# A fused transformer kernel on one core: where the first attention's joins, ternary signs, a weight sum and one tile of values stand

## The chip, the cores and the metric

The kernel runs on one core of a Trainium2 chip. A core has five engines that run side by side, each with its own instruction queue: TensorE (PE, matmuls and transposes; PEld is its loading of weights), VectorE (DVE), ScalarE (ACT), GpSimd (POOL) and SyncE (SP, which issues most of the transfers). An engine works through its queue in order; a wait at the head of a queue holds everything behind it. Matmuls write to PSUM; the other working memory is SBUF.

The metric is the device time of one execution in microseconds (us). Before the change three runs took 573.16, 573.84 and 576.12 us; the median is 573.84.

## What is computed

Four layers, each an attention and a feed-forward, are added onto one residual `x` (2 x 256 rows of 256). Each addition is scaled by the tanh of a gate, and each block's input is layer-normalised. The change touches the first layer and the start of the second:

```python
x = x + jnp.tanh(g_xattn[0]) * _L0_xattn_ref(_layernorm(x, axis=-1), ctx_2048)
x = x + jnp.tanh(g_ffn[0]) * _L0_ffn_ref(_layernorm(x, axis=-1), L0_ffn_W_up, L0_ffn_W_gate, L0_ffn_W_down)
x = x + jnp.tanh(g_xattn[1]) * _L1_xattn_ref(_layernorm(x, axis=-1), ctx_2048, L1_xattn_Wq, L1_xattn_Wk, L1_xattn_Wv, L1_xattn_Wo)
```

The first attention has 16 heads per batch entry and no weights: the queries are slices of the normalised `x`, the keys and values slices of the context. The first feed-forward has ternary weights:

```python
scale = jnp.mean(jnp.abs(w)) + EPS
q = jnp.clip(jnp.round(w / scale), -1.0, 1.0) * scale
...
hidden = jax.nn.silu(up) * gate
return jnp.einsum('bse,de->bsd', hidden, wd)
```

Three weight matrices (up, gate, down) are so reduced to signs of -1, 0 or 1 and one scale each. The second attention has 16 heads of width 128 with query, key, value and output weights.

## The kernel before, in words

`x` is held as four tiles of 128 rows (n = 0 to 3). The first attention runs as a pipeline of 18 steps s, four for each tile (n = s // 4): in each step TensorE computes scores (`l0_scores`, L450), ScalarE takes their exponentials (L456), and TensorE multiplies the exponentials of the step before with the values (`l0_values`, L464). TensorE's instructions are kept in the order of the text by `in_turn`. VectorE's and GpSimd's in this stage are kept in the order of the text too, each in its own list, by `inline` with `line` and `pool_line`, which tie each instruction behind the one before it.

A tile's values come in two halves, each in a PSUM tile of its own; there are two such buffers, so a new half waits until an older one has been read. `l0_join` (L473 for the first half, L475 for the second) brings the halves together in SBUF on VectorE, two instructions each. Then `l0_exchange` (L479) swaps parts of it between partitions with one matmul, and `l0_finish` takes a reciprocal of the result (L485), multiplies and adds to `x` (L489, L280). `norm_stats` follows for the feed-forward's layernorm (L217, L218 on VectorE, L219, L220 on GpSimd), and `norm_apply` (L236) writes the normalised row tile `xn0`.

The ternary weights are prepared between these steps. `ternary_sum` (L339, VectorE) sums the absolute values of one weight matrix over a 128 x 2048 tile; a matmul with ones (L344) adds over the partitions, and `ternary_scale` (L348 to L350) makes the scale and the bounds. `ternary_below` (L360, GpSimd) compares half a matrix with the lower bound; `ternary_signs` (L367, VectorE) compares it with the upper bound and subtracts. So there are six signs, two for each matrix, each 128 x 1024. Before the change they are made in pairs: after the first joins of tiles 1, 2 and 3, ahead of these tiles' second joins. The sum of the down weights (the third) stands ahead of tile 1's first join.

After the last step comes `l1_values_of(0, ...)`: the values of the second attention's first group of four heads, in eight tiles (two matmuls each, L277, and a copy by ScalarE, L564). They depend on the context and the weights alone. Seven are in the text ahead of the feed-forward; the eighth stands behind the feed-forward's norm. In `ternary_ffn` the normalised tiles are transposed on TensorE (L248) and each is split into a high and a low part (`split`: L778, L780 on VectorE, L779 on ScalarE). Then come the matmuls with the signs, silu (L804), product (L805), the split of the product (L372 VectorE, L373 ScalarE, L374 GpSimd) and the matmuls with the down signs (L793). The result is transposed (L816) and added to `x` (L818).

The second attention starts with two heads' keys (L277, copied at L573), the norm of `x` (`norm_pair`, then L236), its transposes (L248, copied at L834 by ScalarE into `xT`), the queries of the first heads and the first scores. The transposes of both norms, and some of the key products (L696), share two PSUM buffers, `ps_tr`. Where the text does not tie instructions, a scheduler orders those of an engine.

All weights live in twelve slots of one SBUF tile, `slab`. The down weights lie in slot 4, up and gate in slots 10 and 11. `load_group(2)` and `load_group(3)` (L101, on SP's queue) bring the second attention's third and fourth weight groups into slots 4 to 7 once these are read for the last time.

Of the kernel before, what the change touches and what calls it, by code (L numbers as in the profile page):

```python
# [22 lines left out]
ALU = mybir.AluOpType  # L23
# [26 lines left out]
def flamingo(ctx: ExitStack, tc: tile.TileContext, a: dict, out: bass.AP):  # L50
    nc = tc.nc
# [53 lines left out]
    l0_w = [load(10, "l0_up"), load(11, "l0_gate")]  # L105
# [71 lines left out]
    def behind(i, j, reason):  # L177

        tc.add_manual_dep(i.ins, j.ins.name, mybir.DependencyInfo(
            mybir.DependencyClass.NoSync, mybir.DependencyReason.DATA), reason=reason)  # L180
# [24 lines left out]
    def inline(i, line=line):  # L205
        if line:
            if line[-1] is not None:
                behind(i, line[-1], "in the order of the text")
            line[:] = [i]
        return i  # L210
# [24 lines left out]
    def norm_apply(n, xn, stats):  # L235
        inline(nc.vector.tensor_scalar(xn[:, n, :], x[:, n, :], *stats, ALU.subtract, ALU.mult))  # L236
# [16 lines left out]
    def tokens(t, n):  # L253
        return t[:, n // 2, :, n % 2 * P : (n % 2 + 1) * P]
# [80 lines left out]
    signs, scales, bounds, parts = [], [], [], []  # L335

    def ternary_sum(w):
        part = small.tile([P, 1], F32, tag="tq", name="tq_part")
        inline(nc.vector.tensor_reduce(part, w, AX.X, ALU.add, apply_absolute_value=True))  # L339
        parts.append(part)  # L340
# [19 lines left out]
            inline(nc.gpsimd.tensor_scalar(t, wi, sc[:, 2:3], None, ALU.is_lt), pool_line)  # L360
            below.append((wi, sc, t))

    def ternary_signs():
        for _ in range(2):
            wi, sc, t = below.popleft()
            signs.append(q4.tile([P, 1024], F32R, tag="q4", name="signs"))
            inline(nc.vector.scalar_tensor_tensor(signs[-1], wi, sc[:, 1:2], t, ALU.is_gt, ALU.subtract))  # L367

    def halves(hi, lo, v):

# [126 lines left out]
    for s in range(18):  # L497
        n = s // 4
        if s < 16:
            es[s] = l0_scores(n, s // 2 % 2, s % 2)  # L500
        if s < 2:

            in_turn(nc.tensor.matmul(busy, lhsT=ones, rhs=ones, start=True, stop=True))

        if s % 4 == 2 and n or s == 17:
            done = n - 1
            l0_exchange(mixed[done], acc[done, 1], done == 1)
        if 1 <= s <= 16:
            m, i, half = (s - 1) // 4, (s - 1) // 2 % 2, (s - 1) % 2
            if half == 0:  # L510
                acc[m, i] = ps_acc.tile([P, 2, D], F32, tag="acc", name="acc")
            l0_values(m, i, half, es.pop(s - 1), acc[m, i][:, 0, :])
        if s == 0:
            ternary_sum(l0_w[0])
            ternary_sum(l0_w[1])
        if s == 3:
            behind(nc.scalar.activation(tg, graw, AF.Tanh), exps[-3], "with the table of exponentials")
            p = acc[0, 0][:, 1, :]
            for w in range(2):
                in_turn(ternary_total(p[:, w : w + 1], w))  # L520
            for w in range(2):
                ternary_scale(p[:, w : w + 1])
            ternary_below(0)
            value_columns(1)
            queries([2], rest[:1])
        if s % 4 == 2 and n or s == 17:
            r = l0_finish(done, acc[done, 1], mixed[done], done == 1)
            stats[done] = norm_stats(done)
            if done == 0:
                ternary_sum(l0_w[2])  # L530
            inline(nc.gpsimd.tensor_add(all_t, all_t, sums.pop(0)), pool_line)
            l0_pool = inline(nc.gpsimd.tensor_add(all_r, all_r, r), pool_line)
            if done < 2:
                ternary_below(done + 1)
        if s % 4 == 2 and s < 16:
            mixed[n] = q2.tile([P, 2, D], F32, tag="q2", name="mixed")
            l0_join(0, acc[n, 0][:, 0, :], mixed[n])
            if n == 0:
                rest = [norm_stats(m) for m in (2, 3)]
            else:  # L540
                ternary_signs()
        if s % 4 == 0 and s:
            l0_join(1, acc[n - 1, 1][:, 0, :], mixed[n - 1])
            if n == 1:
                queries([3], rest[1:])
            if n > 1:
                norm_apply(n - 2, xn0, stats[n - 2])
    norm_apply(3, xn0, stats[3])
    line.clear()
    pool_line.clear()  # L550
    l0_psum.close()
# [6 lines left out]
    def l1_values_of(g, tiles):  # L558
        v = slab[:, 8 + 2 * (g % 2) : 10 + 2 * (g % 2), :].rearrange("p s (m c) -> p (s m) c", m=4)
        for mt in tiles:  # L560
            p = mm()
            chain(p, [(ctxT[:, mt // 4, k, mt % 4 * P : (mt % 4 + 1) * P], l1_w[g][2][:, k, :])
                      for k in range(2)])
            nc.scalar.copy(v[:, mt, :], p)  # L564
        return v

    def l1_keys_of(h):
        kT = q4.tile([P, B * M], F32, tag="q4", name="kT")
        for b in range(B):
            p = mm()  # L570
            chain(p, [(l1_w[h // 4][1][:, k, (h % 4) * HD : (h % 4 + 1) * HD], ctxT[:, b, k, :])
                      for k in range(2)])
            nc.scalar.copy(kT[:, b * M : (b + 1) * M], p)  # L573
        return kT


    v_next = l1_values_of(0, range(7))

# [190 lines left out]
    def ternary_ffn():  # L771


        xs = [q4.tile([P, B, 2, 256], F32R, tag="q4", name="xs") for _ in range(2)]

        def split(n, tr):
            top = q1.tile([P, 2, P], F32, tag="q1", name="topx")
            nc.vector.tensor_scalar(top.bitcast(I32), tr.bitcast(I32), -4096, None, ALU.bitwise_and)  # L778
            nc.scalar.copy(tokens(xs[0], n), top)  # L779
            nc.vector.tensor_sub(tokens(xs[1], n), tr, top)  # L780

        norm_tiles(split, xn0)
        l1_values_of(0, [7])
        s2 = small.tile([P, 1], F32, tag="s2", name="s2", bufs=1)
        nc.vector.tensor_mul(s2, scales[1], scales[2])
        nc.vector.tensor_mul(s2, s2, gf(0))
        outs = [ps_acc.tile([P, T], F32, tag="acc", name="outT") for _ in range(2)]

        def l0_down(c, h):
            w = signs[4 + c // 4].rearrange("p (c d) -> p c d", d=D)[:, c % 4, :]  # L790
            for dh in range(2):
                for i in range(2):
                    nc.tensor.matmul(outs[dh], lhsT=w[:, dh * P : (dh + 1) * P], rhs=h[:, i, :],  # L793
                                     start=(c == 0 and i == 0), stop=(c == 7 and i == 1))

        ps = {}
        for c, _, ts in by_batch(FCH):
            if c not in ps:
                ps[c] = mm(), mm()
            for w, p in zip((0, 2), ps[c]):  # L800
                chain(p[:, ts], [(signs[w + k][:, c * P : (c + 1) * P], batch(h, k, ts)) for k in range(2) for h in xs])
            if ts.stop == T:
                s = q2.tile([P, T], F32, tag="q2", name="silu")
                nc.scalar.activation(s, ps[c][0], AF.Silu, scale=scales[0])  # L804
                nc.vector.tensor_mul(s, s, ps[c][1])  # L805
                h = q4.tile([P, 2, T], F32R, tag="q4", name="hT")
                halves(h[:, 0, :], h[:, 1, :], s)
                later(lambda c=c, h=h: l0_down(c, h), 1)
        flush()
        for dh in range(2):  # L810
            p = outs[dh]
            o = q2.tile([P, T], F32, tag="q2", name="o0")
            nc.scalar.copy(o, p)
            tr = ps_tr.tile([P, NT, P], F32, tag="tr", name="tr")
            for n in range(NT):
                nc.tensor.transpose(tr[:, n, :], o[:, n * P : (n + 1) * P], ident)  # L816
            cols = x[:, :, dh * P : (dh + 1) * P]
            nc.vector.scalar_tensor_tensor(cols, tr, s2, cols, ALU.mult, ALU.add)  # L818
# [3 lines left out]
    ternary_ffn()  # L822
    l1_w += [load_group(2), load_group(3)]
    keys = deque(l1_keys_of(h) for h in range(2))


    line.append(None)
# [76 lines left out]
    for g in range(4):  # L904
        v, oTs = v_next, []
        if g < 3:
            v_next = values_of[g + 1]
        for hl in range(4):
# [15 lines left out]
            for b in range(B):  # L924
                es, by_ones, t = l1_scores(b, qT, kT, h > 13)
# [179 lines left out]
    last = norm_stats(NT - 1)  # L1105
# [67 lines left out]
    halves = slice(0, 2), slice(2, 4)  # L1173
# [94 lines left out]
    last = nc.scalar.activation(prob, lgt, AF.Exp, scale=-1.0)  # L1268
# [19 lines left out]
    t, u = rtile(), place  # L1288
# [20 lines left out]
    for n in range(NT):  # L1309
# [9 lines left out]
    _, owners = nc.values_load_multi_w_load_instructions(  # L1319
        owner_i[0:1, :], engines=[mybir.EngineType.SP], min_val=0, max_val=E - 1,  # L1320
        skip_runtime_bounds_check_because="a count, cut at 7")
# [10 lines left out]
    top = rtile((P, NT))  # L1332
    inline(nc.vector.reduce_max(top, prob, axis=AX.X))
    t = rtile()
# [221 lines left out]
    es, t = l3_exps(0, ps3[0])  # L1556
# [909 lines left out]
```

## Time and profile before

The profile is of one execution, which took 572.92 us; the span from its first to its last instruction is 571.2 us. TensorE's granted clock was 0.999 of full.

| engine | busy us | share of the span |
|---|---|---|
| PE | 553.1 | 97% |
| PEld | 401.0 | 70% |
| DVE | 371.9 | 65% |
| ACT | 178.7 | 31% |
| POOL | 216.4 | 38% |

Busy time of each engine in the stretches that the change touches, in us:

| stretch (us from the start) | what runs there | PE | DVE | ACT | POOL |
|---|---|---|---|---|---|
| 27 to 35 | first attention, tile 1 ends | 6.30 | 7.43 | 6.30 | 7.67 |
| 35 to 44 | tile 2 | 9.00 | 8.53 | 6.70 | 6.30 |
| 44 to 53 | tile 3 | 7.27 | 8.58 | 3.58 | 8.92 |
| 53 to 66 | values tiles, norm of the feed-forward | 13.00 | 5.80 | 4.75 | 6.76 |
| 66 to 92 | first feed-forward | 26.00 | 11.72 | 13.65 | 12.04 |
| 92 to 99 | norm of the second attention | 6.06 | 5.10 | 3.06 | 4.70 |

A line of the timeline gives the start, the duration (from the first start to the last end where instructions are merged, x4 for four of them), the engine, the line of the kernel, the operation, output<-input by the program's names and, in brackets, how long the engine had been idle before it and what ended that. One matmul instruction on fp32 data shows as two records. In the chain of work that ended last each piece is a start, a length, an engine, a tile's name and a line. "L12" is line 12 of the kernel.

### The profile page before, as it was taken

Reading aid. Unit: us, or ns where it says so; the run is one execution under the profiler, and the core shown is the slowest. Engines: PE = TensorE matmul, PEld = TensorE weight load, DVE = VectorE, ACT = ScalarE, POOL = GpSimd, SP = SyncE. Lnnn points to the kernel's source line nnn. Section 1 sums busy time; section 2 is a strip of 40 time slices with the busy share of each in tenths; the row PEclk is TensorE's granted clock in tenths of the full one; section 3 lists DMA queues with packets and bytes.
Section 4 is the critical chain, followed back from the end, with each engine's and each line's share of the span. In section 5 each row is a group of like instructions: output and inputs, shape, how many; then the busy total and the mean of one; then the engine's idle time right before and its main releaser. Section 6 shows DMA issues by size and latency. Waiting matters only on the chain.

```text
span 571.2 us, 8750 instructions
## 1 busy us (share of the span) xinstructions
PE 553.1 (97%) x3300; PEld 401.0 (70%) x3300; DVE 371.9 (65%) x744; ACT 178.7 (31%) x329; POOL 216.4 (38%) x368
## 2 busy tenths in 40 slices
PE   8988999999999999999999999999999999999996
PEld 6553675778788787887878786887775555884445
DVE  6998444677867888588885895675567434563323
ACT  5874543422222222123222221331323221432221
POOL 3787456626332464134342344702022001252151
PEclk9999999999999999999999999999999999999999
DMA  7904200002002100102032324272020899704013
GB/s 294 412 18 188 107 0 1 0 1 74 1 0 75 43 32 1 37 37 75 0 118 104 117 94 158 75 239 75 0 75 2 338 419 415 170 33 129 18 53 116
DMA packets 15528, 59.15 MB, mean 104 GB/s; under 512 B 2653, under 2 KB 5924, under 8 KB 11846
## 3 DMA queue, kind: packets, MB, share of 16 engines
q1 hardware_dynamic: 13430, 53.70, 25.7%
q0 software_dynamic: 1472, 4.28, 2.3%
q8 instruction: 28, 0.46, 0.3%
q10 hardware_dynamic: 576, 0.53, 0.3%
q14 instruction: 22, 0.18, 0.1%
HBM read 53.70 MB, written 5.25 MB: 103 GB/s over the span
## 4 chain that ended last, share of the span: by engine, by line
PE 84%; DVE 8%; POOL 3%; issue 2%; ACT 1%; DMA 1%; SPq 0%; POOLq 0%; DVEq 0%; ACTq 0%
PE mm L277 22%; PE acc L277 18%; PE mm_t L646 4%; PE mm L658 4%; PE mm L1369 4%; PE mm_t L696 4%; PE mm L646 3%; PE mm_t L658 3%; PE mm L696 3%; PE acc L766 2%; PE s L450 2%; PE mm L1700 2%; PE acc L1390 2%; PE acc L1722 2%; PE acc L464 2%
## 5 line engine op out<-in xcount | busy, mean ns | idle before, releaser
L854 ACT ACTIVATE e<-mm 128x512 f32<-128x512 f32 x64 | 38.0, 597 | 115.0 <-PE mm L277 112.4
L873 DVE RECIPROCAL r<-acc 128x256 f32<-128x256 f32 x32 | 56.2, 1757 | 20.7 <-PE acc L277 20.7
L277 PE MATMUL mm<-qT,kT 128*128 128x256 f32 x256 | 61.1, 380 | 0.0
L277 PE MATMUL acc<-e,slab 128*128 128x256 f32 x256 | 60.5, 379 | 0.0
L277 PEld LDWEIGHTS acc<-e,slab 128*128 128x128 f32 x256 | 48.6, 190 | 9.2 <-issue 2.9
L875 POOL TENSOR_TENSOR all_t<-all_t,t 128x256 f32<-128x256 f32 x32 | 24.1, 753 | 80.4 <-DVE t L859 80.4
L277 PEld LDWEIGHTS mm<-qT,kT 128*128 128x128 f32 x256 | 47.7, 190 | 9.4 <-issue 2.9
L876 POOL TENSOR_TENSOR all_r<-all_r,r 128x256 f32<-128x256 f32 x32 | 23.3, 728 | 56.4 <-DVE r L873 56.4
L277 PE MATMUL mm<-xT,slab 128*128 128x256 f32 (+1 forms) x132 | 38.7, 442 | 0.3 <-DVE k L998 0.3
L456 ACT ACTIVATE slab<-s 128x1024 f32<-128x1024 f32 x32 | 30.9, 1021 | 8.5 <-PE s L450 7.9
L858 DVE TENSOR_TENSOR t<-e,e 128x512 f32<-128x512 f32 x32 | 22.9, 716 | 15.0 <-ACT e L854 14.4
L219 POOL TENSOR_TENSOR rstd<-mv,eps_ln 128x1 f32<-128x1 f32 x26 | 6.4, 245 | 68.0 <-DVE mv L218 68.0
L277 PEld LDWEIGHTS mm<-xT,slab 128*128 128x128 f32 x132 | 24.2, 190 | 10.4 <-issue 7.1
L277 PE MATMUL acc<-slab,oT 128*128 128x256 f32 x128 | 29.4, 381 | 0.5 <-DVE oT L874 0.4
L277 PE MATMUL mm<-slab,ctxT 128*128 128x512 f32 x64 | 29.0, 594 | 0.0
L280 DVE SCALAR_TENSOR_TENSOR x<-acc,tg,x 128x256 f32<-128x256 f32 x28 | 13.5, 481 | 23.6 <-PE acc L277 19.8
L277 PEld LDWEIGHTS acc<-slab,oT 128*128 128x128 f32 x128 | 23.7, 190 | 4.9 <-DVE oT L874 1.2
L864 ACT CAST th<-t 128x256 fp32r<-128x256 f32 x28 | 11.3, 405 | 45.4 <-DVE t L862 45.4
L1369 PE MATMUL mm<-slab,xsT 128*32 128x512 f32 x192 | 22.8, 596 | 0.2 <-ACT xsT L1324 0.2
L865 POOL TENSOR_TENSOR th<-t 128x256 fp32r<-128x256 f32 x28 | 20.5, 732 | 5.6 <-DVE t L862 4.6
L236 DVE TENSOR_SCALAR xn<-x,mv,rstd 128x256 f32<-128x256 f32 x28 | 14.0, 507 | 10.4 <-POOL rstd L220 10.0
L450 PE MATMUL s<-slab,ctx_nat 32*128 32x256 f32 x256 | 20.2, 401 | 0.1
(405 smaller groups left out, 1172.2 us busy)
## 6 DMA issues: line engine op xcount, KB each, us to landing
slab<-in_l_gu_all SPq DMA_DIRECT2D x16, 1024.0 KB, 5.2
slab<-in_l_all SPq DMA_DIRECT2D x4, 2048.0 KB, 10.5
slab<-in_l_dn_all SPq DMA_DIRECT2D x4, 1024.0 KB, 5.1
slab<-in_l_dn_all SPq DMA_DIRECT2D x8, 512.0 KB, 10.0
slab<-in_l_gu SPq DMA_DIRECT2D x4, 704.0 KB, 12.5
ctx_nat<-in_ctx SPq DMA_DIRECT2D x4, 512.0 KB, 8.0
slab<-in_l_up SPq DMA_DIRECT2D x2, 1024.0 KB
slab<-in_l_gate SPq DMA_DIRECT2D x2, 1024.0 KB, 10.3
```

The costliest lines, as they stand in the source:

```text
L277: inline(nc.tensor.matmul(dst, lhsT=lhsT, rhs=rhs, start=(i == 0), stop=(i == len(pairs) - 1)), pe_line)
L450: in_turn(nc.tensor.matmul(ps[j // 2][:, j % 2, k, :], lhsT=ctx_nat[rows, b, hf, c * P : (c + 1) * P], rhs=qm[rows, n, i, :], start=True, ...
L456: exps.append(nc.scalar.activation(es[d].rearrange("p j k q -> p (j k q)"), ps[d].rearrange("p j k q -> p (j k q)"), AF.Exp))
L646: nc.tensor.matmul(dst, lhsT=w, rhs=t, start=True, stop=True)
L658: nc.tensor.matmul(t[:, i, :], lhsT=w, rhs=b, start=True, stop=True)
L696: nc.tensor.matmul(dst[:, j, :], lhsT=t[:, j * P : (j + 1) * P], rhs=w, start=True, stop=True)
L854: nc.scalar.activation(e, s, AF.Exp, scale=HD ** -0.5)
L858: nc.vector.tensor_add(t, es[0], es[1])
L873: nc.vector.reciprocal(r, acc[:, 1, :])
L875: nc.gpsimd.tensor_add(all_t, all_t, t)
L876: nc.gpsimd.tensor_add(all_r, all_r, r)
L1369: inline(nc.tensor.matmul(ps[j * BLK : (j + 1) * BLK, :], lhsT=xsT[k][:, (4 * q + j) * BLK : (4 * q + j + 1) * BLK], rhs=gu2[:, home(q, j) ...
```

## The change

Five edits, all of order:

- Tile 1: the sum of the down weights moves from ahead of the first join to behind it. The two signs that followed that join are no longer made there.
- Tile 2: the pair of signs behind its first join is now the first pair (up weights).
- Tile 3: no signs between its joins. One sign (gate weights, first half) is made after its second join and the normalisation of tile 2, another (second half) after the normalisation of tile 3.
- The two signs of the down weights are made in `ternary_ffn`, behind the last instruction of the last split.
- Six of the eight values tiles stand ahead of the feed-forward's norm instead of seven, the seventh behind it, and the eighth after the keys of the second attention's first two heads.

```diff
-    def ternary_signs():
-        for _ in range(2):
+    def ternary_signs(halves, last=None):
+        for _ in range(halves):
             wi, sc, t = below.popleft()
             signs.append(q4.tile([P, 1024], F32R, tag="q4", name="signs"))
-            inline(nc.vector.scalar_tensor_tensor(signs[-1], wi, sc[:, 1:2], t, ALU.is_gt, ALU.subtract))
+            i = inline(nc.vector.scalar_tensor_tensor(signs[-1], wi, sc[:, 1:2], t, ALU.is_gt, ALU.subtract))
+            if last:
+                behind(i, last[0], "the norm is waited for")
...
             r = l0_finish(done, acc[done, 1], mixed[done], done == 1)
             stats[done] = norm_stats(done)
-            if done == 0:
-                ternary_sum(l0_w[2])
             inline(nc.gpsimd.tensor_add(all_t, all_t, sums.pop(0)), pool_line)
...
             if n == 0:
                 rest = [norm_stats(m) for m in (2, 3)]
-            else:
-                ternary_signs()
+            elif n == 1:
+                ternary_sum(l0_w[2])
+            elif n == 2:
+                ternary_signs(2)
         if s % 4 == 0 and s:
             l0_join(1, acc[n - 1, 1][:, 0, :], mixed[n - 1])
             if n == 1:
                 queries([3], rest[1:])
             if n > 1:
                 norm_apply(n - 2, xn0, stats[n - 2])
+            if n == 4:
+                ternary_signs(1)
     norm_apply(3, xn0, stats[3])
+    ternary_signs(1)
...
-    v_next = l1_values_of(0, range(7))
+    v_next = l1_values_of(0, range(6))
...
+        last_split = []
+
         def split(n, tr):
             top = q1.tile([P, 2, P], F32, tag="q1", name="topx")
             nc.vector.tensor_scalar(top.bitcast(I32), tr.bitcast(I32), -4096, None, ALU.bitwise_and)
             nc.scalar.copy(tokens(xs[0], n), top)
-            nc.vector.tensor_sub(tokens(xs[1], n), tr, top)
+            last_split[:] = [nc.vector.tensor_sub(tokens(xs[1], n), tr, top)]
 
         norm_tiles(split, xn0)
-        l1_values_of(0, [7])
+        l1_values_of(0, [6])
+        ternary_signs(2, last_split)
...
     ternary_ffn()
     l1_w += [load_group(2), load_group(3)]
     keys = deque(l1_keys_of(h) for h in range(2))
+    l1_values_of(0, [7])
```

## The prediction

> **What bounds the kernel now.** I read three views: the busy line of the page, the chain of work that ended last (what the end time hangs on), and the timelines of single engines around each place where that chain leaves TensorE. The page first:
>
> ```profile
> PE 553.1 (97%) x3300; PEld 401.0 (70%) x3300; DVE 371.9 (65%) x744; ACT 178.7 (31%) x329; POOL 216.4 (38%) x368
> ```
>
> TensorE (PE) has work for 97% of the span, and the chain lies on it for 84%, on VectorE for 8%, so a gain must come from its few gaps. The chain in time order (start, us, what) shows one in the first attention:
>
> ```profile
> 27.16 2.17 DVE tq_part L339
> 29.33 0.45 DVE mixed L473 x2
> 29.78 0.25 issue
> 30.03 2.80 DVE signs L367 x2
> 32.83 0.80 DVE mixed L475 x2
> ```
>
> The joins (L473, L475) feed TensorE; the weight sum (L339) and the signs (L367) stand ahead of them on VectorE (DVE), and nobody needs these two so early. The chain leaves TensorE in the same way for signs at 48.35 (3.09) and the join at 51.44. TensorE's own timeline (start, us, operation; idle before it and who ended that idleness):
>
> ```profile
> 28.68 1.15 PE L450 MATMUL s<-slab,ctx_nat 32*128 32x256 f32 x16
> 30.26 1.07 PE L464 MATMUL acc<-slab 128*32 128x256 f32 x16 [0.43 <-DVE mixed L473]
> 31.26 1.15 PE L450 MATMUL s<-slab,ctx_nat 32*128 32x256 f32 x16
> 33.67 0.70 PE L479 MATMUL acc<-mixed,swap 128*128 128x256 f32 x2 [1.27 <-DVE mixed L475]
> ...
> 49.03 1.98 PE L277 MATMUL mm<-slab,ctxT 128*128 128x512 f32 x4
> 52.28 0.70 PE L479 MATMUL acc<-mixed,swap 128*128 128x256 f32 x2 [1.27 <-DVE mixed L475]
> ```
>
> Three waits, all ended by a join; tile 3's joins are the last of these. Tile 2's signs (38.75, two in 2.94) cost nothing: its exchange at 43.18 did not wait.
>
> **The change, part by part.** The instruction lists of the two kernels differ in VectorE's places of one sum and six signs, and in the place of one values tile (two matmuls, shown as 4 records, and one ScalarE copy). GpSimd's list and SP's keep their order; nothing is added or removed.
>
> *Joins first.* (1) Tile 1's first join may run at 27.1, straight after the statistics, and ends by 28.0; the values matmuls then follow the scores at 28.68 + 1.07 = 29.75 (1.07 is the step where nothing waits, 21.60 to 22.67), not at 30.26: 0.51 gained. (2) The sum then runs 28.0 to 30.2, the second join to 31.0. The exchange is due after one values block (1.00) and one scores block (1.07), 29.75 + 2.07 = 31.82, so it no longer waits. Before, it came 33.67 - 31.26 - 1.07 = 1.34 after its turn: 1.34 gained. The exponentials don't step in: step 9's run 29.92 to 31.86 and are used after the exchange, 32.6. (3) Tile 3's second join needs only the last values matmuls, which end about 49.1 less the 1.85 already gained, 47.3, and ends by 48.2; the exchange is due one values tile after that block, at 49.03 + 1.72 - 1.85 = 48.90. Before: 52.28 - 50.75 = 1.53 late: 1.53 gained. Sum 3.38 (the row's own idle figures, taken from modelled ends, give 2.97; that is the lower end).
>
> *What the signs now stand before.* The third sign precedes tile 3's reciprocal, the fourth follows the last normalisation. Tile 3's chain, reciprocal to normalised row (53.02 to 58.19, 5.2 us), starts about 50.1 in the new time and ends about 55.2; its transposes come at 60.4, since TensorE has values tiles until then. That cover is 5 us; without it each sign would cost its 1.3.
>
> The fifth and sixth come after the last split, ahead of the feed-forward's first product (L805). Rows there:
>
> ```profile
> 66.37 0.74 DVE L780 TENSOR_TENSOR xs<-tr,topx 128x256 fp32r<-128x256 f32 x2
> 69.02 0.69 DVE L805 TENSOR_TENSOR silu<-silu,mm 128x512 f32<-128x512 f32 x1 [1.91 <-ACT silu L804]
> ...
> 70.25 1.30 POOL L374 TENSOR_TENSOR hT<-silu,top 128x512 fp32r<-128x512 f32 x1 [7.03 <-DVE top L372]
> ```
>
> VectorE is idle 1.91 before L805. A sign that nothing holds up takes 1.28, and the next starts 1.19 after it (38.75, 39.94); two occupy 2.38, from 67.03 to 69.41 on the old clock: the product is 0.39 late. Queued behind it are the truncation (L372), GpSimd's low half (L374) and then TensorE's L793 (first matmul at 71.61), whose second matmul, 0.23 later, at 71.84, needs that half. The half ended at 71.55, for the second chunk at 73.20 against a need at 73.42, so 0.16 to 0.23 of slack remains once about 0.06 of signalling is taken off. Stall 0.39 - 0.16, about 0.25. Ends: nothing (VectorE starts them in a gap), and 0.9 if the pair takes 3.02, as at 48.35.
>
> [...] Rows: of the six signs three take 1.60 to 1.90 with GpSimd at work beside them, three 1.27 to 1.28, and GpSimd's additions (L531, L532) take 1.65 and 1.71 beside signs, 0.73 alone. [...]
>
> *The values tile.* Six of the eight tiles, not seven, are computed ahead of the norm's transposes. Each is 4 records at 0.429 (24 records from 52.98 in 10.30): 1.72 off TensorE's path there, for rows 0 to 2 have been normalised long before the transposes at 63.12, and row 3 about 5 us before its own.
>
> It comes back in the second attention's norm, after five key matmuls. TensorE's rows there:
>
> ```profile
> 95.85 0.60 PE L248 MATMUL tr<-ident,xn 128*128 128x128 f32 x4
> 97.04 0.41 PE L248 MATMUL tr<-ident,xn 128*128 128x128 f32 x2 [0.58 <-ACT xT L834]
> 97.77 0.41 PE L248 MATMUL tr<-ident,xn 128*128 128x128 f32 x2 [0.33 <-DVE xn L236]
> 98.02 0.60 PE L696 MATMUL mm_t<-slab,ctxT 128*128 128x256 f32 x2
> 98.64 1.98 PE L277 MATMUL mm<-xT,slab 128*128 128x512 f32 x4
> ```
>
> and ScalarE's there:
>
> ```profile
> 96.05 0.59 ACT L573 COPY kT<-mm 128x512 f32<-128x512 f32 x1 [1.05 <-PE mm L277]
> 96.54 0.66 ACT L834 COPY xT<-tr 128x256 f32<-128x256 f32 x2
> ```
>
> TensorE idles 0.91 here, less than the tile's 1.72. In these rows' time: the tile runs 95.85 to 97.57, transposes 0 and 1 to 98.01. ScalarE copies the tile at 97.77 (0.2 after its last matmul, as at 63.32), with the transposes' copies queued behind it: xT 0 at 98.26 to 98.63, xT 1 to 98.92. Two PSUM buffers hold transposes, so the third waits for xT 0 (98.76, 0.13 later, as 96.91 to 97.04), the fourth for xT 1 (99.05). The key matmul behind them (98.02, 0.43) needs a buffer of the same pair, so xT 2 (0.44 after its transpose: 99.20 to 99.57): 99.70 to 100.13. The queries then start at 100.13, not 98.64: 1.49 lost. Ends: 0.81 (the tile fills the 0.91) and 2.21 (no idleness filled, and the 0.49 of the copy added); a gain is excluded, as the matmuls run there.
>
> *Transfers.* The load of the third weight group (the last L101) overwrites slot 4, which the last two signs read. It moves from 51.5 to about 64.5 on SP's queue; behind it is only a load that issues at 130.1. Its first reader is GpSimd's sum at 137.99; with the slowest landing of such a load (18.0) it lands by 83. Cost nothing, 55 us of cover.
>
> *Sum:* 3.38 + 1.72 - 0.25 - 1.49 = 3.36 gained. The profiled execution took 572.92, 0.92 below the median of 573.84: it would give 569.6; against the median, 570.5.
>
> **The rivals.** B: the tile fills the second norm's gap. For it: the trace shows 0.91 idle there; against: ScalarE's queue order. Price 0.81, gain 4.04: 569.8. C: the last signs meet GpSimd and run as at 48.35. [...] Stall 0.9, gain 2.71: 571.1. [...] D: the exchanges are no longer late through VectorE but through ScalarE's exponentials. For it: each step holds two of about 1.02 against TensorE's 2.07; against: ScalarE idled 2.22 before step 11's. It decides once under 0.02 of the 3.38 is left; then 573.9, no faster. E, the slower side: the third group's load arrives after its reader. Place SP's queue, price one for one; the reader comes at 134.6 in the new time, a landing at 138 uses up the gain and one at 141 makes 0.5% (576.7), 76 us after the issue where 18.0 is the longest seen. For it only that its issue moves by 13 us.
>
> **How the numbers follow.** About 0.5% (2.9 us) is what a measurement of this kernel can tell from no change; its three runs span 573.16 to 576.12. Forecast 0.58 (570.5, own range 569.8 to 571.2, of which three quarters lie under 570.97), B 0.14, C 0.13, D 0.10, E and the like 0.05. Faster: 0.43 + 0.14, 0.57. Slower: E 0.05 and a third of D, 0.08. Same: 0.35. The unknown prices give 2.97 + 1.72 - 0.9 - 2.21 = 1.58 at the least and 3.38 + 1.72 - 0.81 = 4.29 at the most, 572.3 to 569.5. With the runs' scatter the range is 569.3 to 573.0; it leaves out D and E, 0.15.
>
> **What would show it.** Right: no idle at TensorE ahead of the exchanges of tiles 1 and 3, L464 in the step between unidle, the first transposes of the feed-forward's norm near 58.0, its first L793 near 66.5 with the second matmul waiting 0.1 to 0.3 for GpSimd, the first queries near 95.3. Wrong: an idle gap of over 0.5 ended by an exponential, signs of 1.6 or more after the split, a wait on the third group's load, or queries whose distance from the x update differs from 7.4 (now 5.9, 92.73 to 98.64).

## The result and the profile after

Six runs of the changed kernel took 570.11 to 571.83 us, median 571.08; six of the kernel before beside them 573.13 to 576.12, median 574.14. The ratio is 0.9936, 95% interval 0.9912 to 0.9959: about 3.1 us faster, where 3.36 had been forecast. The profiled execution took 570.11 us with a span of 568.4 (before 572.92 and 571.2), at the same granted clock, 0.999.

In the changed kernel the lines of the code are a few numbers further down: the joins are now L475 and L477, scores L452, values L466, the exchange L481, the feed-forward's product L813, GpSimd's low half of its split L376, the down matmuls L801, the copies of the values tiles L569 and of the second norm's transposes L843 (the runs further down differ by a line or two). From the page, the busy line and the chain that ended last:

```profile
PE 553.2 (97%) x3300; PEld 401.6 (71%) x3300; DVE 371.9 (65%) x744; ACT 178.5 (31%) x329; POOL 214.6 (38%) x368
...
PE 91%; DVE 4%; POOL 2%; ACT 2%; issue 1%; DVEq 0%; POOLq 0%; ACTq 0%
```

The work is the same; the chain now lies on TensorE for 91% of the span instead of 84%, and on VectorE for 4% instead of 8%. TensorE's timeline in the first attention (start, us, engine, line, operation; idle before it in brackets):

```profile
28.76 1.15 PE L452 MATMUL s<-slab,ctx_nat 32*128 32x256 f32 x16
29.84 1.07 PE L466 MATMUL acc<-slab 128*32 128x256 f32 x16
30.84 1.37 PE L452 MATMUL s<-slab,ctx_nat 32*128 32x256 f32 x16
32.14 0.70 PE L481 MATMUL acc<-mixed,swap 128*128 128x256 f32 x2
...
47.49 1.98 PE L277 MATMUL mm<-slab,ctxT 128*128 128x512 f32 x4
49.31 0.60 PE L481 MATMUL acc<-mixed,swap 128*128 128x256 f32 x2
```

None of the three waits is left: no bracket stands at these values (L466) or exchanges (L481). What is new is that the score block at 30.84 takes 1.37, where before the change the block in its place (31.26) took 1.15. Around the feed-forward's first product, all engines:

```profile
60.75 1.30 POOL L597 TENSOR_TENSOR ctx_nat<-ctxT,ctx_nat 128x512 f32<-128x512 f32 x1
...
62.24 2.48 DVE L367 SCALAR_TENSOR_TENSOR signs<-slab,tq_sc,tern 128x1024 fp32r<-128x1024 f32 x2
...
64.63 0.68 DVE L813 TENSOR_TENSOR silu<-silu,mm 128x512 f32<-128x512 f32 x1
...
65.92 1.29 POOL L376 TENSOR_TENSOR hT<-silu,top 128x512 fp32r<-128x512 f32 x1 [3.87 <-PE mm L277]
66.82 1.41 PE L801 MATMUL outT<-hT,signs 128*128 128x512 f32 x4
...
67.26 0.53 PEld L801 LDWEIGHTS outT<-hT,signs 128*128 128x128 f32 x3 [0.48 <-POOL hT L376]
```

The last two signs start 0.19 after GpSimd's last context sum ended (62.05) and take 2.48 together. The product follows them without a pause and GpSimd's low half after it. The first four matmuls with the down signs take 1.41: the loading of weights for the second of them (67.26, PEld) waits 0.48 for that low half. Before the change the same four took 1.07:

```profile
71.61 1.07 PE L793 MATMUL outT<-hT,signs 128*128 128x512 f32 x4
```

TensorE in the second norm:

```profile
91.46 1.88 PE L277 MATMUL mm<-slab,ctxT 128*128 128x512 f32 x4
93.18 0.60 PE L248 MATMUL tr<-ident,xn 128*128 128x128 f32 x4
94.29 0.72 PE L248 MATMUL tr<-ident,xn 128*128 128x128 f32 x4 [0.51 <-ACT xT L843]
95.19 0.70 PE L701 MATMUL mm_t<-slab,ctxT 128*128 128x256 f32 x2 [0.18 <-ACT xT L843]
95.73 1.88 PE L277 MATMUL mm<-xT,slab 128*128 128x512 f32 x4
```

The tile (L277 at 91.46) stands ahead of all transposes; the two idle stretches behind it, 0.69 together, end with ScalarE's copies.

Executions start the first attention up to 0.8 us apart (tile 0's exchange comes at 22.30 to 23.14), so all further times are counted from that exchange. The changed kernel profiled a second time gave the same distance to the second attention's queries, 72.98 us both times:

> The changed kernel once more, on the chip of the other three: ratio 0.994 to 0.995, queries 72.98 us after tile 0's exchange. If the queries' place scatters by more than 0.1 us between executions, the differences of 0.3 to 0.7 us above are not told by single traces.

The way from before to after, in these times:

| point | before | after | gained so far |
|---|---|---|---|
| exchange, tile 1 | 11.00 | 9.39 | 1.61 |
| exchange, tile 3 | 29.61 | 26.56 | 3.05 |
| first transpose, feed-forward's norm | 40.45 | 35.58 | 4.87 |
| first group of four down matmuls | 48.94 | 44.07 | 4.87 |
| second group of four down matmuls | 50.52 | 46.01 | 4.51 |
| update of `x` | 68.65 | 64.18 | 4.47 |
| queries of the second attention | 75.97 | 72.98 | 2.99 |
| last update of `x`, kernel's end | 543.87 | 540.73 | 3.14 |

What is gained by the queries is still there at the end of this execution; the last section says what takes part of it away in others.

### The profile page after: what moved, and what is told of

Read it like the earlier page. It is cut to its first block, busy times and chain, and to the rows that moved or that the text cites. A ratio compares the mean times of both kernels' runs of the same rounds, so it can differ in the third digit from the quotient of the medians.

```text
span 568.4 us, 8750 instructions
## 1 busy us (share of the span) xinstructions
PE 553.2 (97%) x3300; PEld 401.6 (71%) x3300; DVE 371.9 (65%) x744; ACT 178.5 (31%) x329; POOL 214.6 (38%) x368
## 4 chain that ended last, share of the span: by engine, by line
PE 91%; DVE 4%; POOL 2%; ACT 2%; issue 1%; DVEq 0%; POOLq 0%; ACTq 0%
PE mm L277 26%; PE acc L277 18%; PE mm_t L651 4%; PE mm L663 4%; PE mm L1378 4%; PE mm_t L701 4%; PE s L452 3%; PE mm L651 3%; PE mm_t L663 3%; PE mm L701 3%; PE acc L466 3%; PE acc L771 2%; PE mm L1709 2%; PE acc L1399 2%; PE acc L1731 2%; PE outT L801 1%
## 5 line engine op out<-in xcount | busy, mean ns | idle before, releaser
L277 PE MATMUL mm<-qT,kT 128*128 128x256 f32 x256 | 61.1, 380 | 0.0
L277 PE MATMUL acc<-e,slab 128*128 128x256 f32 x256 | 60.5, 379 | 0.0
L277 PEld LDWEIGHTS acc<-e,slab 128*128 128x128 f32 x256 | 48.7, 190 | 9.1 <-issue 2.9
L277 PEld LDWEIGHTS mm<-qT,kT 128*128 128x128 f32 x256 | 47.7, 190 | 9.4 <-issue 2.9
L277 PE MATMUL mm<-xT,slab 128*128 128x256 f32 (+1 forms) x132 | 38.6, 441 | 0.3 <-DVE k L1007 0.3
L277 PEld LDWEIGHTS mm<-xT,slab 128*128 128x128 f32 x132 | 24.3, 190 | 10.0 <-issue 7.1
L277 PE MATMUL acc<-slab,oT 128*128 128x256 f32 x128 | 29.4, 382 | 0.5 <-DVE oT L883 0.4
L277 PE MATMUL mm<-slab,ctxT 128*128 128x512 f32 x64 | 29.2, 594 | 0.0
L277 PEld LDWEIGHTS acc<-slab,oT 128*128 128x128 f32 x128 | 23.7, 190 | 4.9 <-DVE oT L883 1.2
L452 PE MATMUL s<-slab,ctx_nat 32*128 32x256 f32 x256 | 20.4, 401 | 0.1
```

Of the source, the lines that this page charges most:

```text
L277: inline(nc.tensor.matmul(dst, lhsT=lhsT, rhs=rhs, start=(i == 0), stop=(i == len(pairs) - 1)), pe_line)
L452: in_turn(nc.tensor.matmul(ps[j // 2][:, j % 2, k, :], lhsT=ctx_nat[rows, b, hf, c * P : (c + 1) * P], rhs=qm[rows, n, i, :], start=True, ...
```

## The experiments

Each run's gain is read at the queries, against 75.97 of the kernel before; the ratio of times stands beside it. It is formed from all runs and is not the quotient of the two medians, and its interval is mostly wider than what one edit moves.

| run | queries | gain | median us, kernel before beside it | ratio (95% interval) |
|---|---|---|---|---|
| changed kernel, again | 72.98 | 2.99 | 571.10, 575.14 | 0.9938 (0.9914 to 0.9961) |
| e1_tile_only | 75.71 | 0.26 | 576.03, 575.64 | 0.9996 (0.9973 to 1.0020) |
| e2_order_only | 73.24 | 2.73 | 572.42, 575.64 | 0.9929 (0.9901 to 0.9956) |
| e3_sum_back | 73.29 | 2.68 | 571.09, 575.64 | 0.9913 (0.9884 to 0.9943) |
| e4_pair_back | 74.54 | 1.43 | 574.03, 575.64 | 0.9971 (0.9948 to 0.9993) |
| e5_three_signs | 72.90 | 3.07 | 571.62, 575.14 | 0.9939 (0.9918 to 0.9961) |
| e6_tile_between | 72.30 | 3.67 | 570.26, 575.14 | 0.9912 (0.9890 to 0.9935) |
| e7_both | 72.20 | 3.77 | 570.47, 575.14 | 0.9929 (0.9901 to 0.9957) |
| e8_sum_away | 72.67 | 3.30 | 571.33, 575.66 | 0.9932 (0.9909 to 0.9955) |
| e9_all | 71.88 | 4.09 | 570.66, 575.66 | 0.9918 (0.9886 to 0.9950) |

**The tile alone, and the order alone.** e1 is the kernel before with only the tile's edits; e2 is the changed kernel with them undone:

```diff
-    v_next = l1_values_of(0, range(6))
+    v_next = l1_values_of(0, range(7))
...
-        l1_values_of(0, [6])
+        l1_values_of(0, [7])
         ternary_signs(2, last_split)
...
-    l1_values_of(0, [7])
```

> The kernel before with the values tile moved and nothing else. Theory (the tile is worth little): 1.72 us earlier transposes in the feed-forward's norm (63.12 to 61.40), 1.48 lost again in the second attention's norm, so the first queries at 98.4 instead of 98.64 and about 0.24 us gained, ratio 0.9996. Rival (the tile fills the 0.91 us that TensorE idled in the second norm, and so carries a third of the change's gain): queries at 97.7, 0.9 us gained, ratio 0.9984.

> The changed kernel with the values tile back in its old place: joins, sum and signs alone. Theory: the three waits on joins give 2.97 us up to the last exchange, and the last pair of signs costs 0.40 in the feed-forward, so 2.57 us gained, first queries at 96.1, ratio 0.9955. Rival (the tile carries a third): 2.0 us, ratio 0.9965 and queries at 96.6.

The tile alone gains 0.26, the order alone 2.73, and 0.26 + 2.73 is the 2.99 of both: the two do not touch each other. In e1 the first transposes come 1.74 sooner (40.45 to 38.71), and 1.48 is given back in the second norm. Its time is 0.9996 of before (0.9973 to 1.0020), no difference that can be measured. The rival that the tile fills the norm's gap (0.9) falls.

**The sum back.** The down weights' sum again ahead of tile 1's first join:

```diff
             stats[done] = norm_stats(done)
+            if done == 0:
+                ternary_sum(l0_w[2])
...
-            elif n == 1:
-                ternary_sum(l0_w[2])
             elif n == 2:
```

> The changed kernel with the weight sum ahead of tile 1's first join again. Theory: the values matmuls of step 9 wait 0.43 us for that join again (30.3), but the next scores then take 1.08 instead of 1.30, as the exponentials have caught up, so the exchange of tile 1 comes only 0.2 to 0.3 us later than in the changed kernel (32.4 against 32.14): first queries at 96.0. Rival (every wait is worth its full length): the exchange at 32.64, queries at 96.2.

TensorE's timeline of this run:

```profile
28.38 1.15 PE L452 MATMUL s<-slab,ctx_nat 32*128 32x256 f32 x16
29.94 1.07 PE L466 MATMUL acc<-slab 128*32 128x256 f32 x16 [0.41 <-DVE mixed L475]
30.94 1.15 PE L452 MATMUL s<-slab,ctx_nat 32*128 32x256 f32 x16
32.02 0.70 PE L481 MATMUL acc<-mixed,swap 128*128 128x256 f32 x2
```

The wait at the values is back with 0.41, and the values start 0.48 later than in the changed kernel (7.57 against 7.09 behind tile 0's exchange). But the scores behind them take 1.15, not 1.37, and the exchange is only 0.26 later (9.65 against 9.39). So the 0.22 that the score block takes longer in the changed kernel is a wait inside that block, used up when the block comes later. In the changed kernel ScalarE works through four exponentials in a row here:

```profile
30.00 4.02 ACT L458 ACTIVATE slab<-s 128x1024 f32<-128x1024 f32 x4 [0.36 <-PE s L452]
```

The scores write to PSUM tiles that these exponentials read. Taken one by one in the kept traces, the third matmul of the block waits for a count that the exponentials raise. In the changed kernel it starts at 31.08, 0.05 after the first of the four exponentials ended (31.02); in e3 that exponential had ended at 30.65, ahead of the whole block. So it is ScalarE that ends this wait. The kernel before shows the same in other places, where the scores come on time beside four exponentials in a row (PE and ACT):

```profile
26.38 1.37 PE L450 MATMUL s<-slab,ctx_nat 32*128 32x256 f32 x16
...
25.54 4.01 ACT L456 ACTIVATE slab<-s 128x1024 f32<-128x1024 f32 x4 [0.77 <-PE s L450]
```

**The pair back.** Tile 3's two signs again between its joins:

```diff
-            elif n == 2:
+            elif n > 1:
                 ternary_signs(2)
...
-            if n == 4:
-                ternary_signs(1)
     norm_apply(3, xn0, stats[3])
-    ternary_signs(1)
```

> The changed kernel with the gate weights' pair of signs between tile 3's two joins again. Theory: the exchange of tile 3 waits 1.27 us for the second join again (50.7 instead of 49.31) and everything behind it is 1.4 us later: first queries at 97.1, ratio to the kernel before 0.996. Rival (that wait hangs on ScalarE or the last values matmuls, not on the signs): the exchange stays near 49.3.

```profile
50.90 0.70 PE L481 MATMUL acc<-mixed,swap 128*128 128x256 f32 x2 [1.29 <-DVE mixed L477]
```

On TensorE's timeline tile 3's exchange waits 1.29 for its second join, as before the change, and the queries come 1.56 later than in the changed kernel. This pair is the dearest piece among those that were undone one at a time. Tile 1's pair was not put back by itself; of the 1.61 gained at tile 1's exchange the sum accounts for 0.26 (e3), which leaves about 1.35 for that pair.

**One sign fewer behind the split.** The last two signs stop the feed-forward by 0.40. If three signs, the third to the fifth, stand ahead of tile 3's reciprocal, where 4.5 us of cover are left (the next section), one is left behind the split and the product should not be late:

```diff
             if n == 4:
-                ternary_signs(1)
+                ternary_signs(3)
     norm_apply(3, xn0, stats[3])
-    ternary_signs(1)
...
-        ternary_signs(2, last_split)
+        ternary_signs(1, last_split)
```

> The changed kernel with three signs (third to fifth) ahead of tile 3's reciprocal and only the sixth behind the split. Theory (the stall at the first down matmul comes from the two signs being longer than VectorE's gap of 1.91 us): one sign of 1.28 fits, the first four down matmuls take 1.07 again and not 1.41, and the first queries come 0.40 us earlier, 72.6 us after tile 0's exchange (72.98 in the changed kernel). Tile 3's normalised row is then ready near 58.5, 2 us ahead of its transposes. Rival (the three signs make that row late): the second pair of transposes waits, and nothing is gained or time is lost.

It gained 0.08 instead of 0.40. VectorE and GpSimd behind the split in this run:

```profile
61.75 1.29 POOL L596 TENSOR_TENSOR ctx_nat<-ctxT,ctx_nat 128x512 f32<-128x512 f32 x1
...
61.78 2.34 DVE L367 SCALAR_TENSOR_TENSOR signs<-slab,tq_sc,tern 128x1024 fp32r<-128x1024 f32 x1
64.04 0.68 DVE L812 TENSOR_TENSOR silu<-silu,mm 128x512 f32<-128x512 f32 x1
```

The three signs make tile 3's statistics later, so GpSimd's sums behind them are later too, and the last of them begins 0.03 ahead of the sign. The sign takes 2.34 instead of 1.28. This is the prediction's rival C in another kernel: when the sign begins, the sum still runs for 1.26, and the sign takes 1.06 longer. The last section has a GpSimd instruction beside which one sign took 0.32 longer and another took no longer.

**The tile between the transposes.** The tile's matmuls behind the second of the four transposes of the second norm, where TensorE waits for ScalarE anyway, and its copy behind all four copies of `xT`:

```diff
     keys = deque(l1_keys_of(h) for h in range(2))
-    l1_values_of(0, [7])
...
-    norm_tiles(lambda n, tr: nc.scalar.copy(tokens(xT, n), tr), xn)
+    tile7 = mm()
+
+    def take(n, tr):
+        copied = nc.scalar.copy(tokens(xT, n), tr)
+        if n == 1:
+            chain(tile7, [(ctxT[:, 1, k, 3 * P : 4 * P], l1_w[0][2][:, k, :]) for k in range(2)])
+        if n == 3:
+            behind(nc.scalar.copy(v_next[:, 7, :], tile7), copied, "the norm is waited for")
+
+    pe_line.append(None)
+    norm_tiles(take, xn)
+    pe_line.clear()
```

> The changed kernel with the last values tile between the second and third transpose of the second attention's norm, and its copy behind the four transposes' copies on ScalarE. Theory (the tile's price of 1.48 us is the ScalarE copy ahead of the transposes' copies and the two shared PSUM buffers): the tile runs while the first two transposes are copied, queries 0.74 us earlier, 72.2 us after tile 0's exchange. Rival (the price is the tile's own 1.72 us of matmuls, whatever its place): 0.2 us earlier at most.

```profile
91.90 0.60 PE L248 MATMUL tr<-ident,xn 128*128 128x128 f32 x4
92.34 1.88 PE L277 MATMUL mm<-slab,ctxT 128*128 128x512 f32 x4
94.06 0.60 PE L248 MATMUL tr<-ident,xn 128*128 128x128 f32 x4
94.90 0.70 PE L701 MATMUL mm_t<-slab,ctxT 128*128 128x256 f32 x2 [0.24 <-ACT xT L845]
95.44 1.88 PE L277 MATMUL mm<-xT,slab 128*128 128x512 f32 x4
```

On TensorE's timeline of this run the idle stretch ahead of the third transpose (0.51 in the changed kernel) is gone, and the queries come 0.68 sooner. So what the tile costs in the norm hangs on its place and on its copy's place in ScalarE's queue, which this edit moved together: 1.48 ahead of the transposes, 0.80 between them. The 0.80 is what the prediction's rival B (0.81) gave for a tile that fills the gap; it takes this place to get it.

**Both, and then the sum out of the way.** e7 has the edits of e5 and e6. e8 has those of e5, with GpSimd's last context sum put behind the feed-forward's last low half; e9 has e8's and e6's:

```diff
...
-        nc.gpsimd.tensor_sub(t[3], b0_, t[1])
+        return lambda: nc.gpsimd.tensor_sub(t[3], b0_, t[1])
...
-    batch_sums(ctx_sums, ctxT)
+    last_sum = batch_sums(ctx_sums, ctxT)
     ternary_ffn()
+    behind(last_sum(), last_low[0], "not beside the signs")
...
```

> The changed kernel with both of these edits. Theory: they lie in different stages and add up, 1.1 us less than the changed kernel, queries 71.9 us after tile 0's exchange, ratio to the kernel before about 0.993 where the changed kernel has 0.995. Rival (one of them only shifts a wait to the next stage): 0.4 to 0.7 us.

> The kernel with three signs ahead of tile 3's reciprocal and one behind the last split, and GpSimd's last sum over the context (1.29 us) taken from ahead of that sign to behind the feed-forward's last low half. Theory (GpSimd's sum blocked the sign in full there): the sign takes 1.28 again instead of 2.34, the first feed-forward product is no longer late, the first matmul group of the output runs its 4 records at 1.07 instead of 1.21 to 1.41, and the queries of the second attention come 72.6 us after the first exchange, 0.40 sooner than in the changed kernel (72.98). The moved sum costs nothing, since nobody reads it before the second attention. Rival (the sign is long for another reason, the values' copies or its own operands): the sign stays over 2 us and the queries come at 72.9; or the moved sum is in the way of what GpSimd does next and takes 0.3 or more back later.

> The same with the values' tile between the second and the third transpose of the second norm and its copy behind the four copies of that norm. Theory: both gains add up, 0.40 + 0.68, and the queries come 71.9 us after the first exchange, 1.1 sooner than in the changed kernel and 4.1 sooner than in the kernel before; the time is 0.991 to 0.992 of the kernel before. Rival: 72.2, as with the three signs and the tile but the sum left in its place.

e7 gained 0.78 on the changed kernel, which is e6's 0.68 and e5's 0.08, and not the sum expected of both. With the sum away (e8) VectorE and TensorE show:

```profile
62.60 1.28 DVE L368 SCALAR_TENSOR_TENSOR signs<-slab,tq_sc,tern 128x1024 fp32r<-128x1024 f32 x1
64.60 0.69 DVE L813 TENSOR_TENSOR silu<-silu,mm 128x512 f32<-128x512 f32 x1 [0.72 <-ACT silu L812]
...
67.19 1.07 PE L801 MATMUL outT<-hT,signs 128*128 128x512 f32 x4
```

The sign takes 1.28, the product waits for ScalarE's silu and no longer for a sign, and the down matmuls take 1.07. Since nothing but GpSimd's sum was moved against e5, the collision is shown to be the cause there. The queries come 0.31 sooner than in the changed kernel, where 0.40, all of the stall, was expected. The update of `x` also shows 0.31, so the other 0.09 is lost inside the feed-forward; where is not shown. e9 comes out at 71.88 as expected (71.9): 1.10 sooner than the changed kernel, 4.09 sooner than the kernel before. Its median, 570.66, lies below the changed kernel's 571.08, but the intervals of the two ratios overlap, so that it beats the changed kernel rests on the timeline, not on the times; the last section says what hides it.

## Why the prediction came out right, and what in it did not

The forecast was 570.5, the median 571.08; the sum was 3.36, the timeline 2.99. By its steps:

- **Joins, 3.38: measured 3.15.** Steps (1) and (2) were to bring tile 1's exchange 1.85 ahead; it came 1.61 ahead. The sentence that failed is "The exponentials don't step in". It looked at when their results are used, not at when they free the scores' PSUM, and it took 1.07 for the score block from a step in which nothing waits, where the block at 26.38 needs 1.30 until the next instruction (27.68), as the one in question now does (30.84 to 32.14). That is rival D in a small part: 0.22 of the score block, as e3 shows. Step (3) was to gain 1.53. Tile 3's exchange shows 1.44 (3.05 less 1.61). It comes 1.82 after the start of the values tile ahead of it (47.49 to 49.31), not 1.72; from the exchange to the transposes 9.02 then pass, where before less one tile would be 9.12, so these 0.10 come back at once and the full 1.53 arrives: 4.87 - 1.72 = 3.15 at the transposes. e2, in which the tile keeps its place, shows 3.16 there (40.45 to 37.29).
- **Signs 3 and 4, nothing: right.** They took 1.74 each beside GpSimd, and tile 3's normalised row (55.19 to 56.00) was there 4.5 us ahead of the pair of transposes that reads it (60.48), near the 5 us of the text.
- **The stall, 0.25: measured 0.40 at the update of `x`** (4.87 less 4.47). The product's lateness was right, 0.40 for 0.39, and so was the slack behind it: GpSimd's low half came 0.46 later against the matmuls, and the second matmul, which needs it, started 0.22 late. The sum stopped there. Taken one by one, the third matmul, whose weights were loaded behind those that waited, came another 0.11 late, and 0.07 more came behind it, 0.03 up to the second group and 0.04 up to the update of `x`.
- **Rival C** did not happen in the changed kernel: GpSimd's last context sum ended at 62.05 and missed the last two signs by 0.19. That is luck, for, counted from tile 0's exchange, it ended only 1.25 sooner than in the kernel before (there at 61.95 + 1.27 = 63.22, L592), though tile 3's exchange, behind which it comes, stood 3.05 sooner. Two signs took up most of the difference: the third took 1.74 and kept tile 3's reciprocal until 50.85, not 50.1, and the fourth drew out GpSimd's first sum (2.24; 1.27 in e8). e5 shows what the other side of the margin costs, 1.06 on the sign. The prediction's row on the six signs does not say that one of the three short ones, at 31.56, also ran beside GpSimd: a comparison, with no loss (1.27; last section).
- **The tile off the first norm, 1.72, and back in the second, 1.49:** measured 1.71 and 1.48. For the first, the transposes start 10.73 behind tile 3's exchange in e2 (49.21 to 59.94) and 9.02 in the changed kernel. For the second, the replay of ScalarE's queue was right to 0.01 at its end; on the way the third transpose and the key matmul came 0.08 and 0.12 sooner after the tile than replayed, so the last digit is luck. e6 shows that the order of the tile, the transposes and their copies is what makes this price.
- **Rival E:** the third group's loads were issued between 47.64 and 65.12 (one entry on SP's queue), and the first sum that reads them ran at 134.97, behind a wait for a reciprocal and not for a load.

Both misses, 0.23 and 0.15, were in one direction and stayed inside the forecast's own range.

## What to carry to other kernels

Ask of every instruction that stands ahead of one on the path, in an in-order queue, whether anybody needs it that early: here two such places were worth 3 us, while moving work of TensorE's own from one stage to another was worth only what it could fill of the gap there: 0.26 ahead of the transposes, 0.94 (0.26 + 0.68) between them. When a wait goes, replay the next engine's queue with its buffers, because the next limit (here the exponentials that free the scores' PSUM, and a GpSimd sum 0.19 us away from a collision) begins a fraction of a microsecond behind. Where an instruction may collide with another engine's, check the margin with everything ahead of it moved, on both engines.

## What was not expected of the hardware

**TensorE's clock halves in some executions, at a place that the change does not touch.** What e9 gains on the changed kernel is whole (1.11) until 431.4 us of its span; by 435.5 us 1.46 of it is gone. Windows of its profiled execution (length, busy time of PE, PEld, DVE, ACT, POOL, then granted clock, DMA share, GB/s):

```profile
430.00:431.40 1.40, 1.40 (x8) 1.02 (x8) 0.60 (x4) 1.37 (x2) 0.00 (x0) 1.00 0.00 0
431.40:434.70 3.30, 3.30 (x9) 2.26 (x9) 2.44 (x10) 0.31 (x2) 0.00 (x0) 0.50 0.01 2
434.70:436.00 1.30, 1.30 (x6) 0.80 (x4) 1.13 (x7) 0.36 (x1) 0.00 (x0) 0.96 0.00 0
```

For 3.3 us the granted clock is 0.50, and the matmuls of that stretch take 0.59 to 0.78 instead of 0.37 to 0.50. The profiled executions of e2 (twice as long), e4, e5 and e8 show a like stretch between 430 and 440; the seven others, the kernel before and both of the changed kernel among them, do not, though the instructions are the same. The clock records of the kept traces give 3.41 for a stretch and 6.83 for e2's. In the 3.41 us ahead of e9's stretch the profile has TensorE busy for 2.83. Each of the five stretches begins 426.67 us after the record's full clock began. TensorE's longest wait in this part, 0.43 ahead of the router's product, lies 424.6 to 425.8 us behind that beginning in the five executions that are hit, and 422.1 to 424.3 or 426.4 to 426.9 us in the seven that are not. So in these twelve traces the place of this wait, counted from that beginning, tells the executions that are hit from the others; no run varied it, and what lowers the clock is not shown. The 1.46 that a stretch of half clock cost e9 is enough to hide 1.10 us between two kernels' times.

**Of a sign and a GpSimd sum that overlap, the later one loses most of the overlap.** The changed kernel's fourth sign met two of them (timeline, GpSimd and VectorE):

```profile
55.80 0.78 POOL L532 TENSOR_TENSOR all_r<-all_r,r 128x256 f32<-128x256 f32 x1
...
55.92 1.74 DVE L367 SCALAR_TENSOR_TENSOR signs<-slab,tq_sc,tern 128x1024 fp32r<-128x1024 f32 x1
56.54 2.24 POOL L594 TENSOR_TENSOR ctx_nat<-ctxT 128x512 f32<-128x512 f32 x1
```

The first sum still ran 0.66 when the sign began, and the sign took 0.46 more than its 1.28; the sign still ran 1.12 when the second sum began, and that took 0.97 more than the 1.27 it takes in e8. In e5 the overlap was 1.26 and the sign's loss 1.06. So the loss was the overlap less 0.15 to 0.20 each time, and in this place it made GpSimd's sums late enough to reach the last signs by all but 0.19.

It is not so for every GpSimd instruction that a sign overlaps. Before the change the first two signs ran beside GpSimd's comparisons of weights:

```profile
29.45 6.09 POOL L360 TENSOR_SCALAR tern<-slab,tq_sc 128x1024 f32<-128x1024 f32 x2
```

The first comparison ran until 32.29, 2.26 past the start of the first sign (30.03) and 0.73 past that of the second (31.56). These signs took 1.60 and 1.27, so they lost 0.32 and nothing, and the comparison took its usual 2.84. So the loss has to be looked up for each pair of instructions.
